# Layer 1's sort in a two-layer graph network: group ends looked up from both sides at once, and k's exponentials made from one table score

## The chip, the cores and the metric

The kernel runs on one core of a Trainium2 chip. The metric is the device time of one execution in microseconds. The engines are TensorE (PE; its weight loads are shown apart as PEld), VectorE (DVE), ScalarE (ACT), GpSimd (POOL) and SyncE (SP). SP, ACT and POOL also issue DMA transfers.

## What is computed

There are N = 2708 nodes with D = 128 features and a 0/1 adjacency matrix `adj`. Two layers follow one another, each with a residual and a layer norm.

```
# layer 0
deg  = clip(adj.sum(1), 1);  dis = deg ** -0.5
diffusion = dis[:, None] * adj * dis[None, :] @ x - x
attn = softmax(beta * cosine(x) * adj, axis=1)
x    = layernorm(x + diffusion + sigmoid(alpha) * (attn @ x - x))
# layer 1
XW    = x @ W
s_col = XW @ a[:128];  s_row = XW @ a[128:]
den   = exp(leaky_relu(s_row[:, None] + s_col[None, :], 0.01))
num   = adj @ den
att   = where(num != 0, den / num, 0)
x     = layernorm(x + adj @ (att @ XW))
```

The matrix `den` has N x N entries and `num` would be a full product of two N x N matrices. The kernel avoids it. For a column j, exp(leaky_relu(s_row + s_col)) is one of two products, e1(k)·g(j) or e2(k)·g'(j), depending on whether s_row of k is above -s_col of j. If the nodes are sorted by score, the rows k can be added up group by group, and only the pairs inside one group need their own comparison.

## The kernel before, in words

Work goes in four stages. Layer 0's attention takes about the first 232 us. Then come six column strips of layer 0's diffusion (`dif_acc`, to 364 us), each followed by its layer norm, its transposes, its scores and its rows of XW, which are written to the DRAM tensor `xw_d`. Then the sort of layer 1 runs, to 423.6 us. The main loop (`num`, `m_acc`) and the last product H = A · M (`h_acc`) end the kernel.

N is 22 blocks (`NB`) of 128 partitions; a strip is `SW` = 512 columns, the sixth has 148. Node i lies at partition i mod 128, block i div 128, so a score for every node is a tile of 128 x 22. `KEPT` = 3 is the number of strips whose columns of the adjacency matrix are no longer held in SBUF; strips 3, 4 and 5 are (`strips[3]` to `strips[5]`).

**The order.** From the last strip on (`s == NS - 1`) the list `strict` is filled, and every PE and DVE operation that goes through `mm` or `dve` is `pinned` to the order of the program. Those operations all show one line (L161 in the profile; L169 and L175 are the same helpers before that). ACT operations are pinned only where the code says so; the rest, like those of earlier strips, are placed by a planner, and each engine then runs its own list in order. A tile's buffers come from pools, which reuse memory: the pool `tmp` of the sort takes memory that closed pools gave back, and the first write of such a tile waits for the last reader of what lay there.

**Sums over A.** While the sort's steps run on DVE and ACT, PE has gaps. They are filled with the first group's carried term: `tot`, the sum over all nodes of A's columns weighted with `e2_w` (two useful columns of 32, so four such products stand side by side in the four quadrants of the array, partitions 0, 32, 64, 96). `total_early` ("e") loads a row of the first 3 x 512 columns into `nat` by a POOL DMA and multiplies it as four quadrants of 384 columns. `total_kept` ("k") multiplies strips 3, 4 and 5 of one row, held in SBUF, in three quadrants of 512, 512 and 148. Ten of the rows "e" are issued in strips 3 and 4; `fill(pattern)` issues the others and all "k" at fixed places of the strict order.

**The lookup.** The nodes are cut into `NG` = 24 groups of up to `G` = 126. Candidates for the bounds are `Q` = 256 values `theta`, two for each partition. `tally` counts the nodes beyond each candidate for both sorts (`cnt`, summed to `ct`); `spread_out` copies a column to all partitions by a matmul with the identity. `reached` counts, for every candidate, how many others still lie within G of it, in three DVE operations for each half, so `nxt_b[q]` is the number of the candidate at which a group that begins at q ends. Then `ends` is followed step by step, each step a comparison with `bound_no`, a product and a sum in one DVE operation:

```
for g in range(1, NG):
    dve("scalar_tensor_tensor", junk, bound_no, ends[:, g - 1 : g], nxt_b,
        ALU.is_equal, ALU.mult, accum_out=ends[:, g : g + 1])
```

From the ends, `hit` and a matmul with ones make the 24 thresholds `thr`.

**The placing.** `beyond` and `grouped_by` make for each sort ("k" for the rows, "j" for the columns) a one-hot membership `hot` and a running number `run`, and `ahead` adds what lies in earlier partitions. `placed` makes from them the place `at` of each node in its group and the one-hot matrices `onp` (128 x 128 for each block). `valued` scales `hot` by a value per node, 22 small ACT operations for one value. `table` multiplies `onp` and `ons` (slot 0 holds the node's number, the other slots its values) in four quadrants, copies the result to SBUF by ACT (`k_t`, `j_t`) and sums the quadrants with `four` (`k_sel`, `j_sel`). From it come `k_no` and `j_no`, the lists of rows by which POOL gathers rows of A into the ring (`gather`, four buffers `ring0` to `ring3`) and rows of XW (`gather_xw` into `xws`). k's table has three values before: the number, e1 and e2.

**The start of the main loop.** `carried` takes `tot` out of PSUM, `carry_in` puts its parts into rows 0 and 1 of `ring[0]`, `kt` holds e1 and e2 of the sorted nodes, `g_s`, `g_r` and `g_d` the column factors, and `weights` makes the weights `wt` of groups 0 to 3 by ACT; the other twenty come in one DMA on SP. The first `num` matmul then needs `ring[0]` and `wt`.

Of the kernel before, what the change touches and what calls it, by code (L numbers as in the profile page):

```python
# [43 lines left out]
def grouped(  # L44
# [60 lines left out]
    def counted(name, pattern, base, step, size):  # L105
# [23 lines left out]
    row0, row1, rest, head = (  # L129
        const.tile([P, 1], F32, name=n) for n in ("row0", "row1", "rest", "head")  # L130
    )

    four = const.tile([P, 32], F32, name="four")

    def constants():
# [4 lines left out]
        dve("tensor_scalar", row1, node[:, 0:1], 1.0, None, ALU.is_equal)  # L140
        dve("tensor_scalar", rest, node[:, 0:1], 1.5, None, ALU.is_gt)
# [35 lines left out]
    def act(op, *args, **kwargs):  # L177
        if strict:
            pinned("ACT", getattr(nc.scalar, op), *args, **kwargs)
        else:  # L180
            getattr(nc.scalar, op)(*args, **kwargs)  # L181

# [333 lines left out]

    tot = ps_tot.tile([P, 2, SW], F32, name="tot")
    early = KEPT * SW // 4

    def total_early(kb):  # L520
        a = nat.tile([P, KEPT * SW], F32, tag="nat", name="nat")
        nc.gpsimd.dma_start(a, adj_t[ts(kb, P), : KEPT * SW])
        for q in range(4):
            mm(
                nc.tensor.matmul, tot[32 * q : 32 * q + 32, 0, :early], e2_w[:, kb, :],
                a[:, q * early : (q + 1) * early],
                start=(kb == 0), stop=(kb == NB - 1),
                tile_position=(0, 32 * q), skip_group_check=True,
            )

    def total_kept(kb):
        for q in range(NS - KEPT):
            s = KEPT + q
            mm(
                nc.tensor.matmul, tot[32 * q : 32 * q + 32, 1, : width(s)], e2_w[:, kb, :],
                strips[s][:, kb, : width(s)],
                start=(kb == 0), stop=(kb == NB - 1),
                tile_position=(0, 32 * q), skip_group_check=True,
            )

# [8 lines left out]

    kept = [(total_kept, kb) for kb in range(NB)]  # L550
    others = [(total_early, kb) for kb in range(10, NB)]

    def fill(pattern):

        for c in pattern:
            f, kb = (kept if c == "k" else others).pop(0)
            f(kb)


    nxt_b = late.tile([P, Q], F32, name="nxt_b")  # L560
# [11 lines left out]
    def reached(ct_ps):  # L572

        nxt = small.tile([P, 2], F32, tag="nxt", name="nxt")
        for h in range(2):
            more = work2.tile([P, SW], F32, tag="junk", name="more")[:, :Q]
            dve("tensor_scalar", more, ct_ps[:, :Q], ct[:, h : h + 1], None, ALU.subtract)
            dve(
                "scalar_tensor_tensor", more, ct_ps[:, Q:], ct[:, 2 + h : 3 + h], more,
                ALU.subtract, ALU.max,  # L580
            )
            fits = work2.tile([P, SW], F32, tag="junk", name="fits")[:, :Q]
            dve(
                "tensor_scalar", fits, more, G + 0.5, 0.0, ALU.is_lt, ALU.add,
                accum_out=nxt[:, h : h + 1],
            )
        return nxt
# [4 lines left out]
    for s in range(NS):  # L592
# [32 lines left out]
        if strict:  # L625
            fill("ekkk")
# [18 lines left out]
        if strict:  # L645

            dve("tensor_reduce", ct, cnt.rearrange("p s k h -> p (k h) s"), AX.X, ALU.add)
            fill("k")
            ct_ps = spread_out(ct, 4)
            fill("k")  # L650
# [11 lines left out]
        nc.scalar.activation(e2_p[:, mine], low[:, mine], AF.Exp, scale=LEAK)  # L662
        nc.gpsimd.tensor_copy(e2_w[:, mine, 1], e2_p[:, mine])
        if strict:
            nxt = reached(ct_ps)
            nxt_ps = spread_out(nxt, 2)
        pn = ps_mm.tile([P, SW // P, D], F32, tag="mm", name="xw_ps")
# [6 lines left out]
        if strict:  # L674
            nc.scalar.copy(xw[:, :nb, :], pn[:, :nb, :])
            dve("tensor_copy", nxt_b, nxt_ps[:, :Q])
# [6 lines left out]
        if s in (3, 4):  # L683
            for kb in range(5 * s - 15, 5 * s - 10):
                total_early(kb)
    fill("kekkekkekkekkk")
# [20 lines left out]
    e1_p = tab.tile([P, NB], F32, name="e1_p")  # L707
    nc.scalar.activation(e1_p, low, AF.Exp)
# [8 lines left out]
    ons = {"k": (3, None), "j": (2, None)}  # L717
    for name, (m, _) in ons.items():
        t = tmp.tile([P, m, NB, 32], F32, name=name + "_ons")
# [3 lines left out]
    ends = tmp.tile([P, NG], F32, name="ends")  # L723
    dve("tensor_copy", ends[:, 0:1], nxt_b[:, 0:1])
    for g in range(1, NG):
        junk = tmp.tile([P, Q], F32, tag="more", name="junk")
        dve(
            "scalar_tensor_tensor", junk, bound_no, ends[:, g - 1 : g], nxt_b,
            ALU.is_equal, ALU.mult, accum_out=ends[:, g : g + 1],
        )  # L730
    thr_ps = ps_x.tile([P, SW], F32, tag="x", name="thr_ps", bufs=2)
    for h in range(2):
        hit = tmp.tile([P, NG], F32, tag=f"hit{h}", name="hit")
        dve(
            "tensor_scalar", hit, ends, after_node[:, h : h + 1], theta[:, h : h + 1],
            ALU.is_equal, ALU.mult,
        )
        mm(
            nc.tensor.matmul, thr_ps[:, :NG], ones, hit, start=(h == 0), stop=(h == 1)
        )  # L740
    fill("kkk")
    thr = tmp.tile([P, NG + 1], F32, name="thr")
    nc.gpsimd.memset(thr[:, 0:1], -1e9)
    dve("tensor_copy", thr[:, 1:], thr_ps[:, :NG])


    def beyond(name, v):

        gt = tmp.tile([P, NG + 1, NB], F32, name=name + "_gt")
# [3 lines left out]
    def grouped_by(name, gt):  # L753
# [3 lines left out]
        run = tmp.tile([P, NG, NB], F32, name=name + "_run")  # L757
# [9 lines left out]
        return hot, run, ahead, of  # L767

    def placed(name, hot, run, ahead):

        dve(
# [131 lines left out]
    for g in range(2):  # L903
        gather(g)
# [687 lines left out]
```

## Time and profile before

| | |
|---|---|
| median of three runs | 767.89 us (767.18 to 768.49) |
| the profiled execution | 768.18 us, of which 766.5 us are the span of the profile |
| mean granted clock of TensorE | 0.988 |
| attention of layer 0 | to about 232 us |
| diffusion strips, to the end of the last `dif_acc` | to 364.4 us |
| sort, to the first `num` | to 423.6 us |
| main loop, then H | to 650 us, then to the end |

| the sort's steps before | start, us |
|---|---|
| x transposed, last strip (`x_ps`) | 370.56 |
| counts summed (`ct`) | 373.58 |
| `nxt_b` copied | 378.58 |
| first and last of 23 lookups of `ends` | 379.38 and 391.0 |
| `k_gt` | 392.91 |
| k's list of rows (`k_no`) | 405.75 |
| first ring gather on POOL | 406.24 |
| second part of k's table on PE | 406.0 to 410.5 |
| last sum into `tot`, then `carried` | 412.4, 412.56 |
| j's table on PE | 414.4 to 417.2 |
| first `num` | 423.56 |

Times in the profile count from the span's start. A line of the timeline gives the start, the duration, the engine, the line of the code, the operation, output and inputs, and how many instructions are put together; a bracket at its end gives the idle time before it and what ended it. The list of waits gives, for each pair of a waiting operation and a releaser, the microseconds in total, how often, and the longest.

### The profile page before, as it was taken

To read this page: it belongs to the slowest core of one execution; us is meant where nothing else is said; L and a number is where in the kernel's file an instruction comes from. 1 tells how busy PE (TensorE), PEld (TensorE's weight loads), DVE (VectorE), ACT (ScalarE), POOL (GpSimd) and SP (SyncE) were. 2 spreads that over 40 slices of the span, in tenths; PEclk is the share of its full clock that TensorE was granted. 3 is DMA by queue.
4 is the path that set the end of the run, shared out by engine and by line. 5 is a ranking of instruction groups with operands and counts; after the bars stand their busy time and mean duration, and the time that the engine had idled before them with its cause. 6 is when DMAs were issued, how large, how long until landed. Compare 5 with 4: busy or idle time off the path is not lost. (4 is left out here: it accounts for less than half of the span.)

```text
span 766.5 us, 7483 instructions
## 1 busy us (share of the span) xinstructions
PE 732.4 (96%) x2467; PEld 348.5 (45%) x2467; DVE 429.5 (56%) x899; ACT 412.0 (54%) x534; POOL 250.0 (33%) x241
## 2 busy tenths in 40 slices
PE   4999999999999999999899799999999999999995
PEld 2444444734444544445336344444444445544444
DVE  6554454444561533433796899898999981203032
ACT  4375879737841211211246599999999994001000
POOL 3875777867682000001023887111111000000000
PEclk9999999999999999999999999999999999999998
DMA  8989597993306866554369835974444440899970
GB/s 286 387 323 402 216 326 288 375 385 142 139 1 210 296 221 246 192 210 165 104 222 285 270 109 175 222 198 149 159 171 163 142 141 10 258 315 306 310 241 21
DMA packets 58303, 168.30 MB, mean 220 GB/s; under 512 B 3470, under 2 KB 17586, under 8 KB 52418
## 3 DMA queue, kind: packets, MB, share of 16 engines
q1 hardware_dynamic: 43780, 111.56, 41.1%
q0 software_dynamic: 8208, 53.30, 22.2%
q10 hardware_dynamic: 6270, 2.90, 1.3%
q8 instruction: 21, 0.34, 0.2%
q14 instruction: 24, 0.20, 0.1%
HBM read 164.91 MB, written 2.84 MB: 219 GB/s over the span
## 5 line engine op out<-in xcount | busy, mean ns | idle before, releaser
L450 POOL TENSOR_TENSOR total<-total,p_t 128x512 f32<-128x512 f32 (+2 forms) x132 | 155.3, 1177 | 61.3 <-ACT p_t L181 44.1
L161 PE MATMUL num<-ring,wt 128*128 128x512 f32 (+1 forms) x288 | 130.0, 551 | 5.6 <-DVE q L161 4.1
L161 PE MATMUL m_acc<-q,xws 128*128 128x512 f32 x240 | 120.5, 593 | 0.6 <-ACT q L161 0.6
L175 DVE SCALAR_TENSOR_TENSOR z<-sim,gentle,strip 128x512 f32<-128x512 f32 (+1 forms) x111 | 72.9, 673 | 82.0 <-PE sim L169 75.0
L599 PE MATMUL dif_acc<-strip,x_sb 128*128 128x512 f32 (+1 forms) x264 | 104.0, 544 | 0.0
L181 ACT ACTIVATE p_t<-z,shift 128x512 f32<-128x512 f32 (+1 forms) x111 | 68.6, 656 | 52.3 <-DVE z L175 48.5
L169 PE MATMUL att_acc<-p_t,x_sb 128*128 128x512 f32 (+1 forms) x232 | 93.9, 542 | 2.6 <-ACT p_t L181 2.5
L1129 PE MATMUL h_acc<-ring,m_sb 128*128 128x512 f32 x220 | 95.7, 593 | 0.0
L161 DVE COPY q<-num 128x512 f32<-128x512 f32 x144 | 86.5, 614 | 16.3 <-PE num L161 16.2
L169 PE MATMUL sim<-xn_t 128*128 128x512 f32 (+1 forms) x222 | 88.2, 533 | 0.5 <-DVE z L175 0.5
L161 PEld LDWEIGHTS num<-ring,wt 128*128 128x128 f32 x288 | 52.2, 192 | 66.6 <-issue 55.7
L161 DVE SCALAR_TENSOR_TENSOR q<-sr_b,nc_s,q 128x1536 f32<-128x1536 f32 (+1 forms) x48 | 77.4, 1614 | 1.4 <-ACT q L161 1.4
L161 ACT ACTIVATE q<-q,head,rest 128x1536 f32<-128x1536 f32 (+1 forms) x48 | 70.5, 1509 | 8.5 <-DVE ring L161 8.2
L161 PEld LDWEIGHTS m_acc<-q,xws 128*128 128x128 f32 x240 | 45.5, 190 | 57.3 <-issue 56.0
L599 PEld LDWEIGHTS dif_acc<-strip,x_sb 128*128 128x128 f32 x264 | 46.4, 190 | 49.7 <-issue 49.4
L850 POOL DMA_INDIRECT ring<-in_adj_t,k_no x24 | 31.2, 1299 | 109.0 <-PE num L161 100.6
L161 ACT ACT_TABLE_LOAD x49 | 62.9, 1283 | 3.6 <-issue 2.8
L169 PEld LDWEIGHTS att_acc<-p_t,x_sb 128*128 128x128 f32 x232 | 39.7, 189 | 54.2 <-ACT p_t L181 28.1
L1129 PEld LDWEIGHTS h_acc<-ring,m_sb 128*128 128x128 f32 x220 | 41.3, 190 | 49.3 <-issue 49.3
L161 ACT ACTIVATE q<-q,c_s 128x1536 f32<-128x1536 f32 (+1 forms) x48 | 62.7, 1354 | 0.3
L169 PEld LDWEIGHTS sim<-xn_t 128*128 128x128 f32 x222 | 39.6, 190 | 40.9 <-issue 34.2
L375 ACT ACTIVATE row<-row 128x2708 f32<-128x2708 f32 x22 | 54.0, 2452 | 4.0 <-DMA row<-in_adj 3.8
(265 smaller groups left out, 654.3 us busy)
## 6 DMA issues: line engine op xcount, KB each, us to landing
strip<-in_adj_t SPq DMA_DIRECT2D x14, 2816.0 KB, 16.8
row<-in_adj SPq DMA_DIRECT2D x22, 1354.0 KB, 7.0
ring<-in_adj_t SPq DMA_DIRECT2D x27, 1024.0 KB, 5.0
nat<-in_adj_t POOLq DMA_DIRECT2D x22, 768.0 KB, 5.0
strip<-in_adj_t SPq DMA_DIRECT2D x3, 1024.0 KB, 10.4
strip<-in_adj_t SPq DMA_DIRECT2D x2, 814.0 KB, 7.0
strip<-in_adj_t SPq DMA_DIRECT2D x1, 1628.0 KB, 11.5
last<-in_adj_t POOLq DMA_DIRECT2D x1, 1628.0 KB, 9.0
```

The lines of the kernel that those rows point to most:

```text
L161: latest[engine] = op(*args, **kwargs)
L169: op(*args, **kwargs)
L175: getattr(nc.vector, op)(*args, **kwargs)
L181: getattr(nc.scalar, op)(*args, **kwargs)
L375: nc.scalar.activation(z[:, :N], z[:, :N], AF.Copy, accum_out=deg[:, ib : ib + 1])
L450: nc.gpsimd.tensor_tensor(total[:r, :v], total[:r, :v], p_t[:r, :v], ALU.add)
L599: nc.tensor.matmul(acc[:, :v], x_sb[:, jb, :], st[:, jb, :v], start=(jb == 0), stop=(jb == NB - 1),)
L850: nc.gpsimd.indirect_dma_start(out=ring[g % RING][P - G :, :], out_offset=None, in_=adj_t[:, :], in_offset=bass.IndirectOffsetOnAxis(ap=k_ ...
L1129: nc.tensor.matmul(acc[:, : h1 - h0], m_sb[:, kb + b, :], a[:, b, h0:h1], start=(kb + b == 0), stop=(kb + b == NB - 1),)
```

## The change

`reached` now takes two DVE operations for each half: `far` holds the second count plus G + 0.5, and the second comparison is multiplied with the first and summed in one operation. Its two results `fits` are also multiplied with `ones`, which gives for each candidate how many others reach it, that is the way back. The upper 64 partitions of `reach_b` hold that mirrored, and eleven steps follow the ends from the first candidate in the lower half and from the last one in the upper half at once. `both` and a matmul put the two halves side by side; the upper thresholds are read in reverse order and kept at or above the middle one.

The exponentials e1 and e2 of the k side are no longer in the table. The table has the number and the score `low`, and two ACT operations make `kt` of it afterwards. So `k_ons` has two slots. Its slot 0 is made by ACT (22 small operations), where DVE made it in one; j's slot 0 is still made by DVE, but ahead of `k_no`. Strip 4's exponential for `e2_w` is made together with strip 5's.

The sums over A are redealt: the first three strips are three quadrants of 512 columns, and the fourth quadrant takes a row of strip 3. The loads after strip 4 are issued by SP, where POOL issued them. The job letters are now "a", "b" and "c". `carried` goes into `k_ons`' buffer, there are six parts instead of seven to carry in, `onp` is made in one operation, and `gather(0)` stands ahead of j's `placed`.

```diff
+    def first_strips(kb, eng):
+        a = nat.tile([P, KEPT * SW], F32, tag="nat", name="nat")
+        eng.dma_start(a, adj_t[ts(kb, P), : KEPT * SW])
+        for q in range(KEPT):
+            sum_part(0, q, kb, a[:, ts(q, SW)], SW)
+    def with_third(kb):
+        first_strips(kb, nc.sync)
+        kept_strip(3, 0, 3, kb)
+    def last_two(kb):
+        kept_strip(4, 1, 0, kb)
+        kept_strip(4, 1, 2, kb + 1)
+        for b in (kb, kb + 1):
+            kept_strip(5, 1, 3, b)
+    def last_three(kb):
+        kept_strip(3, 0, 3, kb)
+        kept_strip(3, 1, 1, kb + 1)
+        last_two(kb)
+    jobs = {
+        "a": [(last_three, kb) for kb in range(0, EARLY_ROWS, 2)],
+        "b": [(with_third, kb) for kb in range(EARLY_ROWS, NB)],
+        "c": [(last_two, kb) for kb in range(EARLY_ROWS, NB, 2)],
+    }
...
-            dve("tensor_scalar", more, ct_ps[:, :Q], ct[:, h : h + 1], None, ALU.subtract)
             dve(
-                "scalar_tensor_tensor", more, ct_ps[:, Q:], ct[:, 2 + h : 3 + h], more,
-                ALU.subtract, ALU.max,
-            )
-            fits = work2.tile([P, SW], F32, tag="junk", name="fits")[:, :Q]
+                "tensor_scalar", more, ct_ps[:, :Q], ct[:, h : h + 1], G + 0.5,
+                ALU.subtract, ALU.is_lt,
+            )
+            fit = work2.tile([P, Q], F32, tag="fits", name="fits")
             dve(
-                "tensor_scalar", fits, more, G + 0.5, 0.0, ALU.is_lt, ALU.add,
-                accum_out=nxt[:, h : h + 1],
-            )
+                "scalar_tensor_tensor", fit, ct_ps[:, Q:], far[:, h : h + 1], more,
+                ALU.is_lt, ALU.mult, accum_out=nxt[:, h : h + 1],
+            )
...
-            fill("ekkk")
+            fill("abb")
...
-            fill("k")
+            fill("b")
             ct_ps = spread_out(ct, 4)
-            fill("k")
+            far = small.tile([P, 2], F32, tag="far", name="far")
+            dve("tensor_scalar", far, ct[:, 2:4], G + 0.5, None, ALU.add)
+            fill("ac")
...
-        nc.scalar.activation(e2_p[:, mine], low[:, mine], AF.Exp, scale=LEAK)
+        if s == NS - 1:
+            mine = slice((s - 1) * 4, s * 4 + nb)
+        if s != NS - 2:
+            nc.scalar.activation(e2_p[:, mine], low[:, mine], AF.Exp, scale=LEAK)
...
             nxt_ps = spread_out(nxt, 2)
+            for h in range(2):
+                mm(
+                    nc.tensor.matmul, nxt_ps[:, Q:], ones, fits[h],
+                    start=(h == 0), stop=(h == 1),
+                )
...
             nc.scalar.copy(xw[:, :nb, :], pn[:, :nb, :])
-            dve("tensor_copy", nxt_b, nxt_ps[:, :Q])
+            dve("tensor_copy", reach_b[:64], nxt_ps[:64, :Q])
+            nc.scalar.activation(
+                reach_b[64:], nxt_ps[64:, Q:], AF.Copy, scale=-1.0, bias=Q + 1.0
+            )
...
             for kb in range(5 * s - 15, 5 * s - 10):
-                total_early(kb)
-    fill("kekkekkekkekkk")
+                first_strips(kb, nc.gpsimd)
+    fill("bacbab")
...
-    e1_p = tab.tile([P, NB], F32, name="e1_p")
-    nc.scalar.activation(e1_p, low, AF.Exp)
...
+    half_g = NG // 2
+    ends = tmp.tile([P, half_g], F32, name="ends")
+    dve("tensor_copy", ends[:64, 0:1], reach_b[:64, 0:1])
+    dve("tensor_copy", ends[64:, 0:1], reach_b[64:, Q - 1 :])
+    for g in range(1, half_g):
         junk = tmp.tile([P, Q], F32, tag="more", name="junk")
         dve(
-            "scalar_tensor_tensor", junk, bound_no, ends[:, g - 1 : g], nxt_b,
+            "scalar_tensor_tensor", junk, bound_no, ends[:, g - 1 : g], reach_b,
             ALU.is_equal, ALU.mult, accum_out=ends[:, g : g + 1],
         )
+    both = tmp.tile([P, NG - 1], F32, name="both")
+    dve("tensor_scalar", both[:, : half_g - 1], ends[:, : half_g - 1], row0, None, ALU.mult)
+    dve("tensor_scalar", both[:, half_g - 1 :], ends, half_on, None, ALU.mult)
+    ends_ps = ps_x.tile([P, SW], F32, tag="ahead", name="ends_ps", bufs=2)
+    mm(nc.tensor.matmul, ends_ps[:, : NG - 1], ones, both, start=True, stop=True)
...
-    dve("tensor_copy", thr[:, 1:], thr_ps[:, :NG])
+    dve("tensor_copy", thr[:, 1:half_g], thr_ps[:, : half_g - 1])
+    dve(
+        "tensor_scalar", thr[:, half_g:NG], thr_ps[:, NG - 2 : half_g - 2 : -1],
+        thr_ps[:, half_g - 2 : half_g - 1], None, ALU.max,
+    )
...
-    k_hot, k_run, k_ahead, k_of = grouped_by("k", k_gt)
-    valued("k", 1, k_hot, e1_p)
-    valued("k", 2, k_hot, e2_p)
-    fill("ekkekkee")
+    k_hot = grouped_by("k", k_gt)
+    fill("bc")
+    k_run, k_ahead, k_of = numbered("k", k_hot)
+    valued("k", 0, k_hot, from_n)
+    valued("k", 1, k_hot, low)
+    fill("c")
     j_gt = beyond("j", vj)
-    k_onp = placed("k", k_hot, k_run, k_ahead)
+    k_own = chosen("k", k_hot, k_run, k_ahead)
+    k_onp = placed("k", k_own)
+    j_hot = grouped_by("j", j_gt)
+    valued("j", 1, j_hot, sc_p)
+    fill("bcb")
     k_tab, _ = table("k", k_onp, [0], banks("x"), P - G)
-    j_hot, j_run, j_ahead, j_of = grouped_by("j", j_gt)
+    j_run, j_ahead, j_of = numbered("j", j_hot)
+    valued_by_dve("j", 0, j_hot, from_n)
+    fill("b")
     k_no = rows_of_table("k", k_tab, G)
-    valued("j", 1, j_hot, sc_p)
-    k_tab, _ = table("k", k_onp, [1, 2], banks("x", "ahead"), between="eee")
+    j_own = chosen("j", j_hot, j_run, j_ahead)
+    k_tab, _ = table("k", k_onp, [1], banks("x"), between="cbb")
...
-    j_onp = placed("j", j_hot, j_run, j_ahead)
-    carried = tmp.tile([P, 2, SW], F32, name="carried")
-    nc.gpsimd.memset(carried, 0.0)
+    carried = tmp.tile([P, 2, SW], F32, tag="k_ons", name="carried")
+    nc.gpsimd.memset(carried[96:, 1, :], 0.0)
...
+    gather(0)
+    j_onp = placed("j", j_own)
+    gather(1)
+
     carry_in(0, 1, by=by_act)
-    for g in range(2):
-        gather(g)
...
-    dve("tensor_scalar", kt[:, 0, :], k_tab[:, 0, :], row0, None, ALU.add)
-    dve("tensor_scalar", kt[:, 1, :], k_tab[:, 1, :], row1, None, ALU.subtract)
+    nc.scalar.activation(kt[:, 0, :], k_tab[:, 0, :], AF.Exp)
+    nc.scalar.activation(kt[:, 1, :], k_tab[:, 0, :], AF.Exp, scale=LEAK)
+    dve("tensor_scalar", kt[:, 0, :], kt[:, 0, :], rest, row0, ALU.mult, ALU.add)
+    dve("tensor_scalar", kt[:, 1, :], kt[:, 1, :], rest, row1, ALU.mult, ALU.subtract)
...
-    carry_in(5, 6, by=by_dve, ps=ps_num)
+    carry_in(5, by=by_dve, ps=ps_num)
```

## The prediction

> **What bounds the kernel now.** I began with the page: busy time by engine, then the chain that ended last. The chain names only the last microseconds, so it says nothing of the sort, which the change touches. Its stage runs from about 362 to 424 us.
>
> ```profile
> span 766.5 us, 7483 instructions
> PE 732.4 (96%) x2467; PEld 348.5 (45%) x2467; DVE 429.5 (56%) x899; ACT 412.0 (54%) x534; POOL 250.0 (33%) x241
> ```
>
> PE's 96% misleads here: between 367 and 412 us most of it is `tot`, filler put between the sort's steps. The waits of 372 to 424 us show who really waits:
>
> ```profile
> ACT k_ons L794 <- DVE k_hot L161: 15.0, 1, 15.0
> ```
>
> ACT stands idle for 15 us until DVE has `k_hot`. So DVE's serial lookup of the ends sets the pace. Its timeline, start first and then duration:
>
> ```profile
> 373.58 0.20 DVE L161 TENSOR_REDUCE ct<-cnt 128x4 f32<-128x24 f32 x1
> ...
> 379.38 0.49 DVE L161 SCALAR_TENSOR_TENSOR junk<-bound_no,ends,nxt_b 128x256 f32<-128x256 f32 x1
> ...
> 379.90 0.48 DVE L161 SCALAR_TENSOR_TENSOR junk<-bound_no,ends,nxt_b 128x256 f32<-128x256 f32 x1
> ...
> 392.91 0.73 DVE L161 TENSOR_TENSOR k_gt<-vk,thr 128x550 f32<-128x550 f32 x1
> ...
> 405.75 0.18 DVE L161 TENSOR_SCALAR k_no<-k_sel 126x24 uint32<-126x24 f32 x1
> ```
>
> One lookup starts 0.528 us after the other and 23 of them take 12.15 us. From `ct` to `k_gt` are 19.33 us. From `k_gt`, which I call g, the first `num` comes at g+30.65:
>
> ```profile
> 423.56 4.78 PE L161 MATMUL num<-ring,wt 128*128 128x512 f32 x12 [1.08 <-ACT wt L161]
> ```
>
> After that PE bounds the kernel to its end (a step of 8.6 us by the start times of later steps), so what moves the first `num` moves the end. ACT's timeline is the one that the change loads more:
>
> ```profile
> 379.03 0.37 ACT L675 COPY xw<-xw_ps 128x256 f32<-128x256 f32 x1 [3.96 <-PE xw_ps L161]
> 379.43 0.37 ACTq L679 DMA_DIRECT2D xw_d<-xw  x1
> 394.42 10.42 ACT L794 ACTIVATE k_ons<-k_hot,e_p 128x24 f32<-128x24 f32 x44 [15.02 <-DVE k_hot L161]
> 404.75 0.33 ACT L794 ACTIVATE j_ons<-j_hot,sc_p 128x24 f32<-128x24 f32 x1
> 404.99 0.24 ACT L811 COPY k_t<-tab_ps 128x128 f32<-128x128 f32 x1
> 405.13 5.07 ACT L794 ACTIVATE j_ons<-j_hot,sc_p 128x24 f32<-128x24 f32 x21
> ```
>
> 44 small activations take 10.42 us, 0.237 each, and the copy `k_t`, on which `k_no` hangs, slips in after the first of the 22 for j.
>
> **What the Trainium skill says.** "TensorE: Matmul & The Clock Gate", Part 1: PE falls to half rate after an idle window of about 3.4 us and needs about 3.4 us of work to come back. The trace agrees. In windows of 0.5 us (PE busy, granted clock, DMA share, GB/s) the clock is half just after a sparse stretch:
>
> ```profile
> 404.50:405.00 0.50, 0.00 (x0) 1.00 0.97 381
> 406.50:407.00 0.50, 0.50 (x20) 0.50 0.78 319
> ```
>
> It stayed at 0.50 from 406.5 to 409.9. The same page, Part 3, says that matmuls on different column tiles run together, in little more than the time of one. Here a row of four 384-wide pieces and two rows with 512-wide ones repeat every 2.36 us, which is 0.64 + 2 x 0.86, the widest piece each: it agrees. "ScalarE: Activation LUTs", What ACT_TABLE_LOAD costs: about 1.28 us; the trace shows 1.28. "DMA: Bandwidth & Descriptors", Anatomy of one DMA — SWDGE (gpsimd) path, gives about 2 us of fixed cost (for GpSimd's queue); `xw_d`, on ACT's queue, takes 1.8 to 2.5 from issue to landing.
>
> **The change part by part.**
>
> *Sums in strips 3 and 4.* Ten rows become three pieces of 512 instead of four of 384. They sit between `dif_acc` matmuls on a PE that is never idle. By the order of the program strip 3's twenty matmuls stood in runs of 3, 9, 1, 3, 4, and the trace gives 0.80+2.05+0.76+0.78+0.78 = 5.17 us. The fifteen now stand in runs of 1, 8, 1, 2, 3. At 0.97 for the first group of a run and 0.86 for each further one (an estimate from 0.64 x 512/384) that is 6.57. That makes +1.4, and as much again +0.1 in strip 4: **+3.0** (bounds +1 if runs overlap `dif_acc`, +4 if a late load adds).
>
> *Tail of strip 5.* Strip 4's e2 exponential goes with strip 5's, so two table loads of 1.28 us leave ACT ahead of `rstd`. With "abb" (about 3.1) in place of "ekkk", PE reaches `x_ps` 4.65 us after `dif_acc`'s end, where it took 6.19: **-1.55** (0 to -2). `ct` comes at +1.45.
>
> *`ct` to the first lookup.* `reached` loses one DVE operation per half, about 0.45 us each. But PE now runs "ac" (about 2.2), the two spreads, and two new 256-wide matmuls of `fits`, estimated at 0.43 each; `reach_b`'s lower half is then DVE's copy, its upper half ACT's, behind DVE's because they share a tile. That brings `reach_b` to about ct+6.3. And the new `ends` tile lies in memory that `xw` had. DVE's first write of it waits for the `xw_d` DMA, which ACT issues only behind the `reach_b` copy: ct+6.65, and 1.8 to land, ct+8.45. First lookup at ct+8.8 instead of 5.80: **+3.0** (+0.5 if the DMA is early, +3.7 at 2.5 us). Behind the waiting write stands everything on DVE.
>
> *Lookups.* 11 instead of 23: 12 x 0.528 = **-6.34**. `both` (two small operations), the matmul `ends_ps` with a wait such as `thr_ps` has (0.58), and one more operation for `thr`: **+1.0** (0.8 to 2). A lookup on 2x64 partitions is taken at the price of a full one.
>
> So `ct` to `k_gt` takes 19.33+3.0-6.34+1.0 = 17.0, and g moves by +1.45-2.35 = **-0.9**.
>
> *`k_gt` to `k_no`.* DVE sheds `k_ons` (0.93). ACT gets it: 22 for from_n, 22 for low, 22 for j, and in the built order the copy `k_t` stands behind all 66. `k_hot` ends at g+1.45; 66 x 0.237 = 15.65, so ACT copies at g+17.2, `k_sel` and `k_no` follow at g+18.0. Before it was g+12.84: **+5.2**. PE has the table ready at about g+11 and then only `k_sel` next in its order: it is idle for 6 us, though there were 4 rows of sums left to do, which stand behind.
>
> *`k_no` to the first `num`.* `ahead` for j stands behind `k_sel`, so `j_run` starts at g+18.4 and `j_onp` ends at g+24.5 (g+20.3 before). PE runs b, k's second table (1.48), c, b, b, to g+23.3; three `carried` copies (1.24) and two exponentials for `kt` (0.35) must end before `in_ps`, and j's table starts at g+25.9. It ends 2.95-3.15 later at g+29.05. From there to `num` it took 6.4 and takes 6.05 (`wt` has one fewer `carry_in` ahead): g+35.1, **+4.5**. If PE comes back at half clock after its idle, as it did at 406.5, 1.6 us more: **+6.1**. I take +5.0: whether the clock falls there is about even, and a part of a slow stretch would pass while `in_ps` waits for ACT.
>
> *Queues.* SP now issues the twelve "b" loads of 768 KB: early, and each behind a free `nat` buffer; 5.0 us to landing when POOL issued them; at zero, covered by the ends loop (+1 if not). On POOL the first ring gather stands behind a memset of `carried` that needs k's second table, so it is issued at g+22 to 23.5 instead of g+13.3. With 7.8 to 10.8 us to landing it arrives by g+33, ahead of `num`: zero (+2 at 18.8 us, seen once). ring2 now stands behind four `xws` gathers: need is 12.0 us after the first `num`, landing at about +12: **+0.3**.
>
> **Sum:** -0.9+5.0+0.3 = +4.4. Against the profiled run's own 768.18 (span 766.5 and 1.68 around it) that is 772.6; this run stood 0.29 above the median of the three, so 772.3.
>
> **The rivals.** *A, likeliest (0.60):* as above, +2.5 to +6.5; ACT's queue eats what the lookup gives. For it speak 15 us of ACT idle that turn into a queue of 66.
> *B, faster (0.13):* the wait for `xw_d` is over by ct+6.6 (-2.2) and the 66 activations cost less, so that `k_t` is copied when the table is there, g+11 to 12.5. Then g moves by -3.1, `k_no` comes no later than g+12.8, and the first `num` stays near g+30.5: 764 to 765.5. It decides from the point where 66 activations take under 11 us, 0.17 each; at 0.237, seen 44 times in a row, they do not.
> *C, much slower (0.18):* half clock through two windows, loads "b" late on SP, or ring0 landing last: +6.5 to +9, 774.5 to 777.
> *D, no difference (0.09):* the sums in strips 3 and 4 cost +1 instead of +3 and the DMA is half as late: +4.4-2.0-1.2 = +1.2, about 769.1.
> That the shorter loop is hidden anyway is excluded: nothing else holds `k_hot`.
>
> **How the numbers follow.** 772.3 is A's. The range 767.0 to 776.0 takes in A and D, and most of C; it leaves out B and C's upper end, not quite 2 in 10. Within 0.2% (1.5 us, about what a measurement of this kernel can tell from no change) lies D: 0.09. Faster: B, 0.13. Slower: A and C, 0.78.
>
> **What would show it.** Right: `dif_acc`'s end 3 us later; the lookup x11, with DVE's wait for DMA `xw_d` of 2 us before `ends`; x66 activations unbroken, then `k_t`; PE idle for 6 us and DVE waiting some 5 us for `k_sel`; POOL's first ring gather after the last k table; the first `num` at 427 to 429. Wrong: `k_no` within 13 us of `k_gt`, or a first `num` before 423.6.

## The result, and the profile after

The change makes the kernel slower: 780.17 us median (779.27 to 783.59, six runs) against 768.41 (767.18 to 772.75, six runs), a ratio of 1.0148 with an interval of 1.0126 to 1.0171, or 11.8 us. Slower was forecast, but only 4.4 us of it, and the time lies outside the range of 767.0 to 776.0. Every ratio in this text leaves out runs more than 1.5% above the fastest of their kernel; only e10 has such runs, six of its twenty.

The profiled execution is the slowest of the six, 783.59 us. From its page:

```profile
span 781.8 us, 7303 instructions
PE 734.7 (94%) x2383; PEld 350.3 (45%) x2383; DVE 421.1 (54%) x876; ACT 410.3 (52%) x532; POOL 236.6 (30%) x229
```

Its span is 15.3 us longer. To place them, the trace is cut at three instructions: the first `dif_acc` (232.91 before, 234.91 after), the first `num`, and the first transpose `rows` after the main loop.

| stretch, us | before | after | difference |
|---|---|---|---|
| start to the first `dif_acc` | 232.91 | 234.91 | +2.0 |
| first `dif_acc` to the first `num` | 190.65 | 196.27 | +5.6 |
| first `num` to the end of the main loop | 228.17 | 235.96 | +7.8 |

The first stretch is all but untouched by the change, and over the profiles of this case it scattered from 231.1 to 236.5 us. So in this profile the change costs 5.6 us in the strips and the sort, and 7.8 us in the main loop, whose code it does not touch.

In the sort the forecast can be read line by line. DVE's timeline (start, duration):

```profile
376.57 0.20 DVE L165 TENSOR_REDUCE ct<-cnt 128x4 f32<-128x24 f32 x1
...
384.30 0.33 DVE L165 COPY ends<-reach_b 64x1 f32<-64x1 f32 x2 [2.10 <-DMA xw_d<-xw]
...
393.37 0.73 DVE L165 TENSOR_TENSOR k_gt<-vk,thr 128x550 f32<-128x550 f32 x1
...
411.46 0.18 DVE L165 TENSOR_SCALAR k_no<-k_sel 126x24 uint32<-126x24 f32 x1 [4.26 <-PE k_sel L165]
```

The lookup begins 8.1 us after `ct` and behind a wait of 2.10 us for the DMA `xw_d`; there are eleven steps. `k_gt` comes 16.8 us after `ct` (19.3 before), but `k_no` comes 18.1 us after `k_gt` (12.8 before). ACT's timeline shows why:

```profile
394.88 5.30 ACT L846 ACTIVATE k_ons<-k_hot,from_n 128x24 f32<-128x24 f32 x22 [12.15 <-DVE k_hot L165]
400.06 5.26 ACT L846 ACTIVATE k_ons<-k_hot,low 128x24 f32<-128x24 f32 x22
405.22 5.24 ACT L846 ACTIVATE j_ons<-j_hot,sc_p 128x24 f32<-128x24 f32 x22
410.48 0.27 ACT L869 COPY k_t<-tab_ps 128x128 f32<-128x128 f32 x1
```

Three times 22 activations, and only then `k_t`. PE had that table by 405.7 and stood idle for 5.07 us. Here are its timeline and the granted clock in windows of 0.5 us (PE busy, clock, DMA share, GB/s):

```profile
404.23 1.50 PE L165 MATMUL tab_ps<-k_onp,k_ons 128*32 128x128 f32 x44 [2.67 <-DVE k_onp L165]
410.80 0.62 PE L165 MATMUL k_sel<-four,k_t 128*126 128x24 f32 x2 [5.07 <-ACT k_t L869]
```

```profile
409.50:410.00 0.50, 0.00 (x0) 1.00 0.00 0
411.50:412.00 0.50, 0.50 (x6) 0.50 0.00 0
416.50:417.00 0.50, 0.50 (x9) 0.50 0.00 0
```

Behind the idle PE runs at half clock from about 410.4 to 417.2 us, for 6.8 us.

The main loop's loss lies at two steps, in PE's timeline:

```profile
453.40 1.10 PE L165 MATMUL num<-ring,wt 128*128 128x512 f32 x2 [2.59 <-DMA ring<-in_adj_t,k_no]
...
494.82 1.15 PE L165 MATMUL num<-ring,wt 128*128 128x512 f32 x2 [4.14 <-DMA ring<-in_adj_t,k_no]
```

`num` waits for the ring gathers of steps 3 and 7, 6.7 us together. In the kernel before it waits for one once, at step 7:

```profile
480.84 1.10 PE L161 MATMUL num<-ring,wt 128*128 128x512 f32 x2 [0.41 <-DMA ring<-in_adj_t,k_no]
```

The rest is a slower clock behind the two waits (a mean of 0.91 between 456 and 468 us and of 0.86 between 492 and 504, where the kernel before has 1.00 from 444 us on). POOL's timeline shows when the gathers were issued:

```profile
418.00 1.13 POOL L916 DMA_INDIRECT ring<-in_adj_t,k_no  x1 [1.06 <-DVE j_onp L165]
...
433.77 1.08 POOL L916 DMA_INDIRECT ring<-in_adj_t,k_no  x1 [0.30 <-issue]
...
485.69 2.14 POOL L916 DMA_INDIRECT ring<-in_adj_t,k_no  x1 [0.30 <-issue]
```

These are step 0's, step 3's and step 7's. Step 3's is waited for until 453.40, 19.6 us after its issue. Step 7's is issued only 9 us ahead of its use. In both kernels it is the thirty-second gather in POOL's list, behind all 24 of `xws`; but here it comes 54.5 us after the first `num`, and in the kernel before 48.7:

```profile
472.29 1.39 POOL L850 DMA_INDIRECT ring<-in_adj_t,k_no  x1 [0.30 <-issue]
```

Two things differ ahead of it. The ring gathers of steps 2, 3 and 4 follow one another, and those of steps 4 to 6 stand earlier in the list. And POOL itself stands still: two gathers of `xws` wait for a ring gather to land, which none does in the kernel before. The line of the list of waits (us in total, times, longest):

```profile
POOL xws L926 <- DMA ring<-in_adj_t,k_no: 8.6, 2, 5.5
```

### The profile page after: what moved, and what is told of

It reads as the page before. It is cut to its first block, busy times and chain, and to the rows that moved or that the text cites. A ratio compares the mean times of both kernels' runs of the same rounds, so it can differ in the third digit from the quotient of the medians.

```text
span 781.8 us, 7303 instructions
## 1 busy us (share of the span) xinstructions
PE 734.7 (94%) x2383; PEld 350.3 (45%) x2383; DVE 421.1 (54%) x876; ACT 410.3 (52%) x532; POOL 236.6 (30%) x229
## 4 chain that ended last, share of the span: by engine, by line
PE 70%; issue 10%; DMA 7%; ACT 5%; DVE 5%; POOL 3%; POOLq 0%; DVEq 0%; ACTq 0%
PE h_acc L1199 12%; PE att_acc L173 11%; PE m_acc L165 10%; PE num L165 10%; PE sim L173 10%; PE dif_acc L628 6%; DMA ring<-in_adj_t,k_no 4%; PE sim L165 2%; PE att_acc L165 2%; POOL xws L926 1%; ACT k_ons L846 1%; ACT q L165 1%; DMA nat<-in_adj_t 1%; DMA x_sb<-in_x 1%; DVE junk L165 1%
## 5 line engine op out<-in xcount | busy, mean ns | idle before, releaser
L165 PE MATMUL m_acc<-q,xws 128*128 128x512 f32 x240 | 122.3, 600 | 0.3 <-ACT q L165 0.3
## 6 DMA issues: line engine op xcount, KB each, us to landing
strip<-in_adj_t SPq DMA_DIRECT2D x14, 2816.0 KB, 16.8
strip<-in_adj_t SPq DMA_DIRECT2D x3, 1024.0 KB, 13.2
```

What stands on the lines that cost most here:

```text
L165: latest[engine] = op(*args, **kwargs)
```

## The experiments

Two theories were tested. **ACT and PE:** the sort loses to ACT's queue, to PE's idle behind it and to the wait for `xw_d`. **POOL's order:** the planner laid the gathers in another order than in the kernel before, and that costs the main loop. The rivals were that PE's sums hold the tail anyway, and that the DMA engines are simply full. "After `k_gt`" and "after the first `dif_acc`" are times read from each kernel's profile.

### e1: j's score activations behind `k_no`

```diff
-    valued("j", 1, j_hot, sc_p)
     fill("bcb")
...
     k_no = rows_of_table("k", k_tab, G)
+    valued("j", 1, j_hot, sc_p)
```

> The changed kernel with one edit: the 22 activations of j's score are put after k_no in the program, so that on ACT the copy k_t of k's first table stands ahead of them (44 activations ahead of it, not 66). My theory (ACT's queue holds k_no, and PE's idle brings the half clock): k_t is copied at about 12 us after k_gt's start instead of 17.1, k_no comes at 12.8 instead of 18.1, PE's idle shrinks from 5 us to under 1, the half clock after it goes, and the first num comes 31 to 32 us after k_gt instead of 37.8: 5 to 7 us less in all, about 774. Rival (PE's sums and loads hold the tail, not ACT): k_no comes early but the last sum into tot stays within 2 us of where it was, and the whole gains 2 us or less.

Measured: 778.39 us (772.6 to 779.84), 1.0101 of the kernel before (1.005 to 1.0153). `k_t` is copied 14.3 us after `k_gt`, `k_no` comes at 15.25, the first `num` at 33.9 instead of 37.8.

```profile
407.06 0.27 ACT L869 COPY k_t<-tab_ps 128x128 f32<-128x128 f32 x1 [2.34 <-PE tab_ps L165]
```

Now ACT waits for PE and not PE for ACT: the table itself took 2.50 us, at half clock for the most part, after PE had waited 2.67 us for `k_onp`. The queue was worth 3.9 us of the first `num` and no more; then PE's sums and its clock take over. The main loop stays at 235.7 us. The whole is 1.8 us below the changed kernel, where 5 to 7 had been expected, and its four runs are spread over 7 us; for the whole the rival, 2 us or less, was nearer.

### e2: all gathers pinned, one ring and one `xws` in each step

```diff
-        nc.gpsimd.indirect_dma_start(
+        pinned(
+            "POOL", nc.gpsimd.indirect_dma_start,
...
     gather(1)
+    gather(2)
...
-    for g in range(2, RING):
+    for g in range(3, RING):
         gather(g)
```

> The changed kernel with all gathers on POOL pinned: ring 0, 1, 2, four of xws, ring 3, and then one ring gather and one of xws in each step; before the edit ring 2 stands behind four of xws, and the gather for step 7 behind eighteen of xws. Theory (POOL's order makes the ring late): the waits of num for a ring gather, 2.6 and 4.1 us in the profile of the changed kernel, and the slow stretch of clock after each go; 4 to 7 us less in the main loop, about 775. Rival (the DMA engines are simply full when four ring gathers, xws and wt come together, whatever the order): the waits stay or move to another step, and the whole gains less than 2 us.

Measured: 780.17 us (779.34 to 781.67), no gain. No `num` waits for a ring gather any more; the waits, in the profile's list for 420 to 650 us, show what does:

```profile
ACT wt L165 <- DMA wt<-g_d: 8.4, 1, 8.4
```

With ring 3 and two more ring gathers issued around it, the transfer of the twenty weights took 26 us to land (21 in the changed kernel, 14 in the kernel before), and the main loop takes 236.5 us. For this order the rival was right: the wait moved.

### e3: sums before `k_sel`, so that PE is not idle

```diff
-    k_tab, _ = table("k", k_onp, [0], banks("x"), P - G)
+    k_tab, _ = table("k", k_onp, [0], banks("x"), P - G, between="bcbb")
...
-    fill("b")
...
-    k_tab, _ = table("k", k_onp, [1], banks("x"), between="cbb")
+    k_tab, _ = table("k", k_onp, [1], banks("x"))
```

> The changed kernel with the last seven jobs of sums moved: four stand between k's first table and k_sel, and none is left between k's second table and its k_sel. ACT's queue is as it was. Theory (PE's idle of 5 us and the half clock behind it cost 3 us of the tail): k_no stays at about 18 us after k_gt, the clock stays full, the last sum ends before j_onp, j's table starts 3 us earlier, and the whole is 2.5 to 3.5 us shorter, about 777. Rival (the loads for these sums come too late to be put there, so k_sel is pushed back): k_no 2 us later or more, and no gain or a loss.

Measured: 770.58 us (766.75 to 774.38), 1.0026 of the kernel before (1.0008 to 1.0045). Some 9.6 us came back, three times what was expected. The first `num` is 2.1 us earlier, somewhat less than forecast: PE's idle ahead of `k_sel` is gone, but the clock did not stay full. It was 0.50 in the windows at 404 and 405 us, behind PE's wait of 2.67 us for `k_onp`. The other 7.8 us come from the main loop, which takes 228.13 us, just what it takes in the kernel before. PE's wait at step 7 and POOL's first gather:

```profile
483.58 1.10 PE L165 MATMUL num<-ring,wt 128*128 128x512 f32 x2 [0.18 <-DMA ring<-in_adj_t,k_no]
```

```profile
410.20 1.13 POOL L915 DMA_INDIRECT ring<-in_adj_t,k_no  x1 [27.35 <-DVE k_no L165]
```

With the sums done by then, the gathers follow `k_no` at once, 16.6 us ahead of the first `num` instead of 13.2, and the planner put ring 2 ahead of `xws` and spread the others. Two things changed at once, start and order; e5, e7 and e8 bear on which of them counts.

### e4: the kernel before with the new lookup alone

Its edit is the diff's part from `reached` to `thr`, in the kernel before, with that kernel's `fill("kkk")`; at its core:

```diff
-    for g in range(1, NG):
+    for g in range(1, half_g):
...
+    mm(nc.tensor.matmul, ends_ps[:, : NG - 1], ones, both, start=True, stop=True)
```

> The kernel before with the new lookup alone: reached in two operations, reach_b, eleven steps from both sides, ends_ps, thr in two parts; sums, exponentials, tables and orders of before. In this one the new ends tile doesn't lie in memory that xw had. Theory: DVE has the ends 4 to 5 us earlier, but PE's list of sums ahead of ends_ps ended at 391.9 in the profile before and isn't shorter, so the matmul ends_ps waits for it; within 1.5 us of the kernel before. Rival (the lookup's gain passes on): k_gt 4 us earlier and 3 to 4 us less in all, about 764.5.

Measured: 767.5 us (764.48 to 775.73), 0.9986 (0.9962 to 1.001): no difference that can be told. DVE's timeline:

```profile
383.92 0.22 DVE L162 TENSOR_SCALAR both<-ends,half_on 128x12 f32<-128x12 f32 x1
388.71 0.51 DVE L162 TENSOR_SCALAR hit<-ends_ps,after_node,theta 128x23 f32<-128x23 f32 x2 [4.56 <-PE ends_ps L162]
```

DVE has the ends in 12 us where it took 18, and then waits 4.56 us for PE, whose list of sums ahead of `ends_ps` is as long as ever. In the kernel before, DVE's chain and PE's list ended within a microsecond of one another. In the changed kernel, where the sums are dealt anew, it is PE that waits at this matmul, so there the lookup does set the pace:

```profile
390.87 0.59 PE L165 MATMUL ends_ps<-both,ones 128*128 128x23 f32 x2 [3.02 <-DVE both L165]
```

### e5: the changed kernel with POOL's order of the kernel before

```diff
+    gather(2)
...
-    for g in range(2, RING):
-        gather(g)
+    gather(3)
+    for g in range(4, 7):
+        gather_xw(g)
...
+            for n in {0: range(7, 11), 1: range(11, 20), 2: range(20, NG)}.get(g, ()):
+                gather_xw(n)
```

Both gathers go through `pinned`, as in e2, and the call in each step is replaced by the last two lines.

> The changed kernel with one edit: POOL's gathers pinned in the order that they have in the kernel before (ring 0, 1, 2, four of xws, ring 3, three of xws, ring for step 4, four, ring for step 5, nine, ring for step 6, four, ring for step 7 and the rest); sort and sums as changed. Theory (the order in which POOL issues ring and xws decides the first eight steps): the time from the first num to the end of the main loop falls from 236 us to 228 to 229.5, no wait of num for a ring gather over 0.5 us, the first num stays where it is; 6.5 to 8 us less than the changed kernel, about 773. Rival (the gathers come later by the later sort, and the DMA engines are full whatever the order): as with the pinned order tried first, the wait only moves, to the DMA wt or another ring gather, and the main loop stays over 233 us.

Measured: 780.01 us (777.26 to 781.62), no clear gain; the main loop takes 234.1 us. Steps 3 and 7 no longer wait, but step 6 does:

```profile
483.69 2.04 PE L165 MATMUL num<-ring,wt 128*128 128x512 f32 x2 [5.01 <-DMA ring<-in_adj_t,k_no]
```

POOL stands still again, 3.7 us in two waits of `xws` gathers for ring gathers. The order alone does not mend it, so the rival was right here: the wait moved.

### e6: `ends` and `junk` in memory of their own

```diff
-    ends = tmp.tile([P, half_g], F32, name="ends")
+    ends = late.tile([P, half_g], F32, name="ends")
...
-        junk = tmp.tile([P, Q], F32, tag="more", name="junk")
+        junk = late.tile([P, Q], F32, tag="more", name="junk")
```

> The changed kernel with ends and junk of the lookup in memory of their own, so that DVE's first write of ends no longer waits for the DMA xw_d. Theory (the wait for xw_d costs 1.5 us of the sort): first lookup 6.3 to 6.6 us after ct instead of 8.1, k_gt earlier by 0.5 to 1.6, since PE's sums ahead of ends_ps end some 3 us before it now and give that much room; first num earlier by as much; with the main loop unchanged 0.5 to 1.6 us less than the changed kernel. Rival (ACT and PE are late anyway, so the time is waited elsewhere): k_gt earlier, first num within 0.3 of where it was.

Measured: first lookup 6.4 us after `ct` instead of 8.1, `k_gt` 2.0 and the first `num` 3.1 us earlier in the profile, but the whole is 780.93 us (778.23 to 783.73), no gain. The profile is of the fastest of the four runs; in it the main loop takes 235.7 us, no longer than in the changed kernel, so it does not show where the other runs lost what the sort gave. As a measure of the wait in the whole this run is inconclusive; e9 repeats it in a kernel whose main loop waits for the ring by less than 2 us.

### e8: the kernel before with POOL's order of the changed kernel

Both gathers are pinned, rings 0 and 1, 2 and 3 stay where the program has them, and

```diff
-            if g + 4 < NG:
-                gather_xw(g + 4)
+            for n in {0: range(4, 6), 1: range(6, 14), 2: range(14, NG)}.get(g, ()):
+                gather_xw(n)
```

> The kernel before with one edit: POOL's gathers pinned in the order that they have in the changed kernel (ring 0, 1, four of xws, ring 2, 3 and for step 4 in a row, two of xws, ring for step 5, eight of xws, ring for step 6, ten of xws, ring for step 7). Theory: the sort stays, first num 190.7 us after the first dif_acc; num waits for ring 3 or the ring of step 7, and from the first num to the end of the main loop it takes 233 to 236 us instead of 228.2; 5 to 8 us slower than the kernel before. Rival (the loss needs the later k_no of the changed kernel): 2 us slower or less.

Measured: 777.21 us (773.51 to 778.3), 1.01 of the kernel before (1.0065 to 1.0136). The main loop takes 235.3 us, and `num` waits for the ring at steps 2 and 7, where the changed kernel waits at 3 and 7:

```profile
437.49 7.83 PE L161 MATMUL num<-ring,wt 128*128 128x512 f32 x12 [2.20 <-DMA ring<-in_adj_t,k_no]
...
486.93 2.04 PE L161 MATMUL num<-ring,wt 128*128 128x512 f32 x2 [5.15 <-DMA ring<-in_adj_t,k_no]
```

This is the converse of e5: the order alone, in a kernel whose `k_no` is early, costs 7.1 us of main loop. Here too POOL stands still, 4.7 us in two waits for ring gathers, and the gather for step 7 comes 54.7 us after the first `num`. The first gather is issued 18.9 us ahead of the first `num`, earlier than in any other run, and that does not help. The rival, that the loss needs the late `k_no`, is refuted.

### e7, e9, e10: the changed kernel mended

e7 joins POOL's order of e5, ACT's of e1 and the memory of e6, and deals the sums to where PE waits:

```diff
-    fill("bc")
+    fill("b")
...
-    fill("c")
+    fill("cc")
...
-    fill("bcb")
+    fill("bcbbc")
...
-    fill("b")
...
-    k_tab, _ = table("k", k_onp, [1], banks("x"), between="cbb")
+    k_tab, _ = table("k", k_onp, [1], banks("x"), between="bb")
```

> The changed kernel with all that the runs so far point to: POOL's order as in the kernel before, j's score activations behind k_no in the program (on ACT one of them goes ahead of k_t), ends in memory of its own, and the sums dealt so that PE is not idle while DVE makes k_onp (b ahead of the running numbers, cc, then bcbbc ahead of k's table, bb after k_sel). Theory: k_gt 157 us after the first dif_acc, k_no at 13 us after k_gt, first num 31 us after it, so first num 188 to 190 us after the first dif_acc against 190.65 in the kernel before and 196.27 in the changed one, main loop 228.2: 764.5 to 767.5, at or below the kernel before. Rival (the 3 us more of sums in strips 3 and 4 and PE's sums in the sort leave nothing of the lookup's gain): within 1 us above the kernel before or slower.

Measured: 765.28 us (761.73 to 771.81), 0.9951 of the kernel before (0.9932 to 0.997): it beats both kernels. DVE's `k_no` and PE's first `num`:

```profile
392.70 0.73 DVE L165 TENSOR_TENSOR k_gt<-vk,thr 128x550 f32<-128x550 f32 x1
...
405.67 0.18 DVE L165 TENSOR_SCALAR k_no<-k_sel 126x24 uint32<-126x24 f32 x1
```

```profile
422.11 4.13 PE L165 MATMUL num<-ring,wt 128*128 128x512 f32 x9 [0.25 <-issue]
```

`k_no` comes 13.0 us after `k_gt` and the first `num` 185.6 us after the first `dif_acc`, 5.0 earlier than in the kernel before; the clock was full in every window of 0.5 us sampled between 404 and 418 us. The main loop takes 228.4 us, with one wait for the ring of 1.8 us, although the first gather is issued no earlier than in the changed kernel (13.3 us ahead of the first `num`). In the whole, 3.9 us remain.

e9 is e7 with `ends` and `junk` back in `xw`'s memory:

```diff
-    ends = late.tile([P, half_g], F32, name="ends")
+    ends = tmp.tile([P, half_g], F32, name="ends")
...
-        junk = late.tile([P, Q], F32, tag="more", name="junk")
+        junk = tmp.tile([P, Q], F32, tag="more", name="junk")
```

> The mended kernel (POOL's order as in the kernel before, j's score behind k_no, sums redealt in time) with ends and junk back in the memory that xw had, so that DVE waits for the DMA xw_d again. Theory (that wait is now on the path, with nothing behind it to hide in): first lookup 8.1 us after ct instead of 6.4, k_gt 1.5 to 2.1 us later, first num as much later, and the whole 1.5 to 2.5 us above the mended kernel, about 767. Rival (as with ends alone in the changed kernel, whose whole did not follow its first num): within 0.7 us of the mended kernel.

Measured: 766.66 us (763.23 to 771.1), 0.9968 (0.9946 to 0.9989). `k_gt` is 2.0 and the first `num` 1.9 us later than in e7. The whole is 1.4 us above, a little less than the theory had, and the two intervals overlap: the wait's price is shown in the sort and only indicated in the whole.

e10 is e7 with POOL's order left to the planner. The calls stand again where the changed kernel has them, and they are no longer pinned:

```diff
-        pinned(
-            "POOL", nc.gpsimd.indirect_dma_start,
+        nc.gpsimd.indirect_dma_start(
```

> The mended kernel with POOL's order left to the planner, which now puts ring 2 ahead of xws but the ring for step 4 straight behind ring 3, three of xws before step 5's, eight before step 6's and nine before step 7's. Theory: with the ring's fill begun early (first gather 16 us or more ahead of the first num) and ring 2 ahead of xws, this order costs little: main loop 228 to 230 us, within 2 us of the mended kernel. Rival (the early ring for step 4 makes wt and ring 3 late as in the first pinned order): a wait of 2 to 5 us for a ring gather or wt, main loop 231 to 235, 3 to 6 us above the mended kernel.

Measured: 770.56 us (761.66 to 775.98), 0.9984 (0.9958 to 1.001); the median of the fourteen runs in the ratio is 767.8. The first `num` is where e7 has it. The theory's premise did not hold: the first gather is issued 13.2 us ahead of the first `num`, not 16 or more. The profiled execution waits for the ring of step 7:

```profile
479.15 1.58 PE L165 MATMUL num<-ring,wt 128*128 128x512 f32 x2 [3.32 <-DMA ring<-in_adj_t,k_no]
```

Its main loop takes 232.2 us, as the rival had it. The whole is 2.5 us above e7 by the fourteen runs and 5.3 by all twenty; the two ratios just overlap (0.9958 here, 0.997 at most in e7), so the price of this order is shown in the profile and only indicated in the whole.

## Why the prediction was wrong in size

**Right, with the sizes named.** Sums in strips 3 and 4: +3.0 forecast, and the end of `dif_acc` is 134.45 us after its start instead of 131.46. (The terms as written make 2.9.) From `ct` to `k_gt` 17.0 forecast, 16.8 measured, in part by luck: the first lookup came 0.7 us earlier than forecast, and what stands between the last lookup and `k_gt` cost 0.5 more. The wait for the DMA `xw_d` is in it, and e6 and e9 show it worth 2 us of `k_gt`. `k_gt` -0.9 forecast, -1.5 measured. ACT's queue of 66: `k_no` at 18.0 forecast, 18.1 measured; `j_onp` ends at 24.5 forecast, 24.6 measured. That the copy stands behind j's 22 is shown by e1, for 3.9 us of the first `num`.

**Too small: the tail from `k_no` to `num`.** I took +5.0, between full and half clock (+4.5 and +6.1). It was +7.2: PE was at half clock for 6.8 us, and the last sum ended 26.0 us after `k_gt`, where the forecast has 23.3 at full clock and, with its 1.6 us for half clock, 24.9. The idle had been foreseen (6 us, 5.07 measured) and its consequence given even odds; what was sized too small is how long it lasts. The half clock cited from the kernel before lasted 3.4 us, from 406.5 to 409.9, and stood behind a stretch in which PE was never idle for more than 0.9 us at a time; that trace therefore did not show an idle window of 3.4 us ahead of it. In e3 it lasted 3.4 us again, but 6.8 in the changed kernel and in e1. An idle of 2.67 us stands ahead of it in e1 and e3, and the same idle in the changed kernel (at 404.23) is followed by the full clock. e7 shows no half clock in that stretch.

**The step that failed: the queues, put at +0.3.** "ring2 now stands behind four `xws` gathers: ... +0.3", and the first gather "arrives by g+33, ahead of `num`: zero". The main loop paid 7.8 us. I had followed POOL's list as far as ring 2 and asked of each gather alone whether it would land in time. For ring 0 and ring 2 the answer was right: neither is waited for. The wait came at steps 3 and 7. Two things were missed, and a third that looks like a cause is none:

- The list beyond. In the changed kernel the ring gathers of steps 2, 3 and 4 follow one another, and those of steps 5 and 6 stand earlier; that could be read from the built order as plainly as ring 2's place. e8 shows that this order by itself costs 7 us of main loop.
- The price of gathers that run together. Rings 2, 3 and the one for step 4 are issued within 4 us (432.4 to 436.3), with `wt` between them, the DMA share is 1.02 to 1.05 from 440 to 456 us, and step 3's gather is waited for 19.6 us after its issue. The price taken, 7.8 to 10.8 us, was the shortest and the median of ten gathers in the kernel before (and from an issue at g+23.5, the latest forecast, 10.8 lead to g+34.3, not g+33). Read one by one, the same profile has 8.5, 13.6 and 16.2 us for the first three, issued within 4 us, and 8.4, 12.1, 18.8 and 20.8 for four issued from 472.3 to 480.7. So 18.8, which the prediction calls seen once, is what a gather behind two others took there. In e2 it is `wt` that comes last.
- The lead of the first gather. It was issued 13.2 us ahead of the first `num` instead of 17.3, behind the memset of `carried`, as forecast. But e7 and e9 have the same lead (13.3 and 13.2) and main loops of 228.4 and 229.0 us, and e8 has 18.9 and loses.

How the bunched gathers turn into the late one of step 7 is in part argued. In every run whose `num` waits for the ring and whose main loop takes 234 us or more (the changed kernel, e1, e5, e6 and e8), gathers of `xws` on POOL wait 3.7 to 8.6 us for ring gathers; in the kernel before, e3, e4, e7 and e9, which take 229 us or less, there is no such wait over 0.3 us. No run removes that wait alone, and e10 loses 4 us without it.

Of the rivals, C came nearest (774.5 to 777, still 3 us short) and named half clock through two windows and a late ring 0 among its causes, with a chance of 0.18; the half clock came, and the ring was late at steps 3 and 7, not at 0. B's premise, that ACT's queue does not bind, is refuted by the 5.07 us of PE's idle and by e1.

**What stays open.** e5 has the order of the kernel before and a lead of its first gather (12.8 us) like that of e9 (13.2), and yet its main loop takes 234.1 us and that of e9 229.0. In e5 the DMA engines were as full but moved 209 to 250 GB/s from 427 to 447 us, which is from 4 us before its first `num` to 16 after, where e9 moved 259 to 305 in the same stretch. No run was made to find out why. So the order is shown to cost the main loop 7 us where the sort is early (e8), and the order of before with the sums dealt anew is shown to mend it (e7, e9); why that order is not enough in the changed kernel's own sort is not known.

## What to carry to other kernels

When a change moves the time at which an index list is ready, follow every DMA of the loop behind it in its queue's built order until the order is again that of the kernel before, and price the transfers together, not one by one. A shortest and a median landing time hide that: list the landings of gathers that were issued close together. A lookup made twice as fast is worth nothing while another engine's list of filler ends with it (e4); shorten or move the filler in the same edit, and to places where that engine would wait (here an idle of 5.07 us was followed by 6.8 us of half clock). Where a queue's order decides, pin it: left to the planner it was another one in the changed kernel, in e3 and in e10. But a good order is not enough by itself, as e5 shows.

## What the runs showed that was not expected

An order that keeps ring gathers from being waited for (e2) made another transfer of that time, `wt`, take 26 us instead of 14 and gained nothing.

A gather of 126 rows landed in 7.8 us in the kernel before when no other ring gather was under way (issued at 463.45), and in up to 20.8 us behind others. And the half clock around k's tables lasted 3.4 us in the kernel before and in e3, and twice that, 6.8 us, in the changed kernel and in e1.

With POOL's order left to the planner the mended kernel was also more scattered: the middle half of the fourteen runs in e10's ratio lies between 766.4 and 771.5 us, that of e7's twenty between 763.7 and 767.0. This is one pair of kernels, and an indication only.
